# Turning the channels of a scan group by the state's number, in a kernel of two state-space layers

## The chip, the cores and the metric

The kernel runs on one core of a Trainium2 chip. The metric is the device time of one execution in microseconds. A profiled execution gives, beside its time, the span of the work on the core and a trace of every instruction and every DMA packet.

## The reference, cut to what matters

The input `x` is 8 images of 384 channels and 32 x 32 pixels, in float32. Four layers follow one another, each `x = x + layer(group_norm(x))`:

- layer 0: a selective scan over the 1024 pixels (Mamba), 768 inner channels, 16 states each;
- layer 1: a filter in the frequency domain of 8 x 8 blocks, a 3 x 3 convolution by channel and a gate;
- layer 2: a layer norm, the same kind of scan as in layer 0, and an MLP of 384 to 1536 to 384;
- layer 3: a 3 x 3 convolution by channel.

The change lies in the scan of layers 0 and 2. For each inner channel `d` and each state `n`:

```
def step(h, inp):                          # t runs over 1024 pixels
    dt_t, B_t, C_t, u_t = inp
    dA = exp(dt_t[..., None] * A)          # A: [768, 16]
    h = dA * h + (dt_t * u_t)[..., None] * B_t[:, None, :]
    y = einsum('bdn,bn->bd', h, C_t)       # sum over the 16 states
```

So `dt` and `dt * u` are the same for the 16 states of a channel, `B` and `C` are the same for all channels, and `A` differs in both. In which order the channels stand while they are scanned does not matter, so long as `A` and the last sum use the same order.

## The kernel before, in words

**Two phases.** `mamba_phase` runs twice, once for layers 0 and 1, and once for layers 2 and 3. Each goes over 16 chunks: 8 images, each in two halves of `T` = 512 pixels. What a scan needs of the first half it finds in `carry` in the second.

**The scan.** A chunk has 768 channels x 16 states = 12,288 rows of 512 pixels. They are done in 48 steps (`PAIRS`), and a step takes two sets of 128 rows: 8 channels x 16 states on the 128 partitions, the state as the slower index, twice. So `g` and `dA` are tiles of 128 x 2 x 512. A phase has 768 steps, both have 1536.

**The replicas.** A row of `dt` has to stand on 16 partitions, once for each state. `front` therefore computes `dt` (L294) and `du = dt * u` (L297) for 128 channels at a time, and writes each to a tile in DRAM with four DMAs on SP's queue (L302), 32 channels each. The tile is `[2, 32, 2, 512]`: block pair `jp`, channel within a block of 32, block within the pair, pixels. One row of a channel is then 2 x 512 float32, 4 KiB. `begin` (L308) reads back 8 such rows (`E8`), each 16 times, with one DMA of 512 KiB (L313): the source has a first dimension of 16 and step 0. There are two reads in a step, `dtr` from `dtd` and `g` from `dud`, on SP's queue. `dtr` has three buffers and `g` seven. `begin` stands four steps ahead of the scan.

**One step.** In the program's order:

- `begin` issues the two replica reads for step t + 4;
- `times` (L325) multiplies `g` by `B` on POOL for step t + 2;
- `decay` (helper line L96) makes `dA = exp(dtr * A)` on ACT, into PSUM, with two buffers, for step t + 1;
- `scan` (L341) runs two scan instructions on DVE for step t;
- `times` again multiplies by `C`, on DVE for even steps and on POOL for odd ones;
- `gather` (L361) sums over the states on PE: a matmul with the 128 x 32 matrix `sely[:, sub, :]`, which adds the 16 partitions of a channel into the channel's row of `y`.

**What runs between.** Three lanes of other work go on in small pieces between the steps: `front` of the next chunk (in-projection, `dt`, the writes to DRAM), `back` of the current one (gate, L374 to L386), and the end of the chunk before (out-projection L399, then layer 1, or the MLP with weights loaded at L684 and L697, or layer 3). Each engine works through its own instructions in order, and SP's queue issues its DMAs in order. The tile framework sets the final order at build time and puts in the waits; in that order DMAs take eight semaphores in turn, so that a DMA on SP also waits for the one that had its semaphore before.

**Order of channels.** `_constants` builds `sely` with a 1 where partition (n, e) belongs to channel `8 * s + e`, and the host arranges `A_log` to match the partitions.

Of the kernel before, what the change touches and what calls it, by code (L numbers as in the profile page):

```python
# [10 lines left out]
F32 = mybir.dt.float32  # L11
# [5 lines left out]
P = 128  # L17
# [4 lines left out]
ND = DI // P  # L22
NS = 16
# [3 lines left out]
T = 512  # L27
# [8 lines left out]

E8 = 8
NSUB = 4  # L40
PAIRS = [(k, s, jp) for k in range(ND) for s in range(NSUB) for jp in range(2)]
NPAIR = len(PAIRS)
PER_K = NPAIR // ND
# [6 lines left out]
def _flat(ap):  # L50
    return ap.rearrange("p a b -> p (a b)")
# [12 lines left out]
def tile_conv_preact_d4(ctx: ExitStack, tc: tile.TileContext, a: dict, out: bass.AP):  # L64
    nc = tc.nc

    const = ctx.enter_context(tc.tile_pool(name="const", bufs=1))
    dram = ctx.enter_context(tc.tile_pool(name="dram", bufs=1, space=DRAM))
# [33 lines left out]
    sely = const.tile([P, NSUB, 32], F32, name="sely")  # L102
# [82 lines left out]
    def mamba_phase(pre, src, normalise, after_out, tail, load_more, after_chunk=None):  # L185
# [4 lines left out]
        A = w["A"]  # L190
# [16 lines left out]
        def front(s):  # L207

            b, c = s["b"], s["c"]
            if c == 0:  # L210
                s["xn"] = load_half(b, 0)
                stats[b] = yield from group_stats(
                    lambda h, k: s["xn"][:, k, :] if h == 0 else load_block(b, 1, k)
                )
            else:
                s["xn"] = load_half(b, c)
            xn = s["xn"]
            for k in range(KC):
                group_norm(xn[:, k, :], xn[:, k, :], k, stats[b])
            yield  # L220
            if normalise:
                yield from normalise(xn)
            u = s["u"] = wk.tile([P, ND, T], F32, tag="u", name="u", bufs=2)
            xt = xt_of[c] = wk.tile([P, ND, 2], F32, tag="xt", name="xt", bufs=2)
            for d in range(ND):
                ps = yield from ps_tile("ps_in")
                for k in range(KC):
                    nc.tensor.matmul(  # L228
                        ps,
                        w["in"][:, k, d * P : (d + 1) * P],  # L230
                        xn[:, k, :],
                        start=k == 0,
                        stop=k == KC - 1,
                    )
                act(
                    u[:, d, :], ps, AF.Identity, scale=vec[:, d, 2:3], bias=vec[:, d, 3:4]
                )
                if c < NCH - 1:
                    act(xt[:, d, :], ps[:, T - 2 : T], AF.Copy)
                for j in (1, 2):  # L240
                    nc.vector.scalar_tensor_tensor(
                        u[:, d, j:T],
                        ps[:, 0 : T - j],
                        vec[:, d, 2 - j : 3 - j],
                        u[:, d, j:T],
                        ALU.mult,
                        ALU.add,
                    )
                ps_done()
                yield  # L250
            if c > 0:

                prev = xt_of[c - 1]
                hal = wk.tile([P, ND, 3], F32, tag="hal", name="hal")
                nc.gpsimd.tensor_mul(
                    hal[:, :, 0:2], prev, vec[:, :, 0:1].to_broadcast([P, ND, 2])
                )
                nc.gpsimd.tensor_mul(hal[:, :, 2:3], prev[:, :, 1:2], vec[:, :, 1:2])
                nc.gpsimd.tensor_add(hal[:, :, 0:1], hal[:, :, 0:1], hal[:, :, 2:3])
                nc.gpsimd.tensor_add(u[:, :, 0:2], u[:, :, 0:2], hal[:, :, 0:2])  # L260
                yield
            act(_flat(u), _flat(u), AF.Silu)
            yield
            ps = yield from ps_tile("ps_x")
            for d in range(ND):
                nc.tensor.matmul(
                    ps[:RX, :], w["x"][:, d, :], u[:, d, :], start=d == 0, stop=d == ND - 1
                )
            dbc = wk.tile([RX, T], F32, tag="dbc", name="dbc")
            act(dbc, ps[:RX, :], AF.Identity, bias=one_row)  # L270
            ps_done()
            yield
            s["bc"] = wk.tile([P, 2, T], F32, tag="bc", name="bc", bufs=2)
            for j in range(2):
                ps = yield from ps_tile("ps_bc")
                nc.tensor.matmul(ps, selbc[:, j, :], dbc[0:DT0, :], start=True, stop=True)
                act(s["bc"][:, j, :], ps, AF.Copy)
                ps_done()
            yield
            s["dtd"], s["dud"] = [], []  # L280
            for d in range(ND):
                ps = yield from ps_tile("ps_dt")
                nc.tensor.matmul(  # L283
                    ps, w["dt"][DT0:RX, d * P : (d + 1) * P], dbc[DT0:RX, :],
                    start=True, stop=True,
                )

                m = wk.tile([P, T], F32, tag="spm", name="spm", bufs=2)
                act(m, ps, AF.Abs)
                act(m, m, AF.Exp, scale=-1.0)  # L290
                act(m, m, AF.Ln, bias=1.0)
                yield
                dt = wk.tile([P, T], F32, tag="dt", name="dt", bufs=2)
                nc.vector.scalar_tensor_tensor(dt, ps, 0.0, m, ALU.max, ALU.add)  # L294
                ps_done()
                du = wk.tile([P, T], F32, tag="du", name="du", bufs=2)
                nc.gpsimd.tensor_mul(du, dt, u[:, d, :])  # L297
                for name, v in (("dtd", dt), ("dud", du)):
                    to = dram.tile([2, NSUB * E8, 2, T], F32, tag=name, name=name, bufs=2 * ND)
                    s[name].append(to)  # L300
                    for j in range(4):
                        nc.sync.dma_start(  # L302
                            to[j // 2, :, j % 2, :], v[32 * j : 32 * (j + 1), :]
                        )
                yield


        def begin(s, i):  # L308
            k, sub, jp = PAIRS[i]

            def replica(of, tag, bufs):
                t = wk.tile([P, 2, T], F32, tag=tag, name=tag, bufs=bufs)
                nc.sync.dma_start(  # L313
                    _flat(t),
                    of[k][jp, E8 * sub : E8 * (sub + 1)].rearrange("e j t -> e (j t)")
                    .unsqueeze(0).to_broadcast([NS, E8, 2 * T]),
                )
                return t

            s["dtr", i] = replica(s["dtd"], "dtr", 3)  # L320
            s["g", i] = replica(s["dud"], "g", 7)
# [154 lines left out]
        for t in range(total):  # L476
            s, i = steps[t]
# [270 lines left out]
def _constants():  # L748

    ch = np.arange(C) // GS
    group = (ch[:, None] == ch[None, :]) / GS
    y, x = np.meshgrid(np.arange(PS), np.arange(PS), indexing="ij")
    rows, spread = [], []
    for l in range(PS // 2 + 1):
        for k in range(PS):
            phase = 2 * np.pi * (k * y + l * x) / PS
            own = l in (0, PS // 2)  # L760
            if own and k in (0, PS // 2):
                basis = [np.cos(phase) / PS]
            elif own and k > PS // 2:
                continue
            else:
                basis = [np.sqrt(2) * f(phase) / PS for f in (np.cos, np.sin)]
            e = np.zeros((PS, PS // 2 + 1))
            e[k, l] += 0.5 if own else 1.0
            e[-k % PS if own else k, l] += 0.5 if own else 0.0
            for v in basis:  # L770
                rows.append(v)
                spread.append(e.reshape(-1))
    basis = np.stack(rows)
    both = np.zeros((2, PS * PS, PS, 2, PS))
    for i in range(2):
        both[i, :, :, i, :] = basis
    both = both.reshape(P, P)
    spread = np.concatenate([np.stack(spread)] * 2)
    selbc = np.zeros((DT0, 2, NS, E8))
    sely = np.zeros((NS, E8, NSUB, 32))  # L780
    for n in range(NS):
        for j in range(2):
            selbc[j * NS + n, j, n, :] = 1.0
        for e in range(E8):
            for s in range(NSUB):
                sely[n, e, s, E8 * s + e] = 1.0
    one = np.zeros((RX, 1))
    one[DT0] = 1.0
    f = np.float32
    return {  # L790
        "c_group": group.astype(f),
        "c_dft": np.ascontiguousarray(both.T).astype(f),
        "c_idft": both.astype(f),
        "c_spread": np.ascontiguousarray(spread.T).astype(f),
        "c_selbc": selbc.reshape(DT0, 2, P).astype(f),
        "c_sely": sely.reshape(P, NSUB, 32).astype(f),
        "c_one": one.astype(f),
    }
# [68 lines left out]
```

## Time and profile before

| | |
|---|---|
| median of 3 runs | 9624.29 us (9611.26 to 9663.54) |
| profiled execution: time | 9647.44 us |
| profiled execution: span | 9645.6 us |
| granted TensorE clock | 0.757 |
| busy: PE, DVE, ACT, POOL | 65%, 65%, 55%, 59% |
| DMA queue of SP (q1) | 1960.22 MB, 82.4% of 16 engines |
| replica reads (L313) | 2 x 1536 DMAs of 512 KB |
| writes of `dtd` and `dud` (L302) | 2 x 768 DMAs of 64 KB |
| HBM, whole span | 1834.06 MB read, 125.83 MB written |

How to read it: an engine's share is the time in which it executes something, over the span. The DMA share is the time that packets took, summed over the 16 DMA engines, over 16 spans; a packet here is one contiguous piece, 4096 bytes in a replica read, and the small ones are the semaphore updates. A wait is the idle time of an engine before an instruction, under the name of what ended it. "Landing" is the time from the issue of a DMA to its completion.

### The profile page before, as it was taken

How to read it: one execution, taken by the hardware profiler on the slowest of the kernel's cores; microseconds unless marked ns; L12 is line 12 of the kernel's file. 1: busy time of each engine (PE TensorE's matmuls, PEld its weight loads, DVE VectorE, ACT ScalarE, POOL GpSimd, SP SyncE). 2: the span in 40 equal slices, each digit the busy share in tenths (PEclk: the TensorE clock that was granted, in tenths of full speed). 3: DMA queues.
4: the chain of work that ended last, by engine and by line, in shares of the span. 5: the costliest groups of instructions: out<-in, count | busy, mean ns of one | idle time of the engine just before them, and what ended most of it. 6: DMA issues, size and time to landing. Idle time of an engine off the chain costs nothing. (4 is left out here: it accounts for less than half of the span.)

```text
span 9645.6 us, 69137 instructions
## 1 busy us (share of the span) xinstructions
PE 6229.8 (65%) x17410; PEld 2463.2 (26%) x17410; DVE 6273.9 (65%) x6854; ACT 5307.2 (55%) x7051; POOL 5730.9 (59%) x3085
## 2 busy tenths in 40 slices
PE   5566665665556666555557766777666776667765
PEld 1112121211212121111113332333323333233333
DVE  4767676676767667675556576665767656676564
ACT  6776765544546454453446555565555655556552
POOL 3765666666566666665255656556565565665653
PEclk7677676777768677776768877787777887778877
DMA  6988878798887879886478888888888998888885
GB/s 170 228 201 203 213 191 207 187 221 195 200 193 195 206 188 223 195 201 165 117 183 210 221 226 212 210 222 221 223 211 214 221 223 219 210 217 222 223 221 139
DMA packets 631865, 1964.65 MB, mean 204 GB/s; under 512 B 86986, under 2 KB 139130, under 8 KB 631468
## 3 DMA queue, kind: packets, MB, share of 16 engines
q1 hardware_dynamic: 631468, 1960.22, 82.4%
q8 instruction: 143, 2.34, 0.1%
q14 instruction: 254, 2.08, 0.1%
HBM read 1834.06 MB, written 125.83 MB: 203 GB/s over the span
## 5 line engine op out<-in xcount | busy, mean ns | idle before, releaser
L325 POOL TENSOR_TENSOR g<-g,bc 128x1024 f32<-128x1024 f32 x2304 | 5371.0, 2351 | 2279.4 <-DMA g<-dud 1201.9
L361 PE MATMUL y<-g,sely 128*32 128x512 f32 x6144 | 2017.6, 792 | 2262.4 <-POOL g L325 1279.2
L96 ACT ACTIVATE dA<-dtr,w_A 128x512 f32<-128x512 f32 x3072 | 2081.9, 687 | 2324.9 <-DVE g L325 1363.9
L96 ACT ACT_TABLE_LOAD x1201 | 1540.9, 1283 | 164.1 <-DMA dtr<-dtd 52.9
L341 DVE TENSOR_TENSOR_SCAN dA<-dA,carry,g 128x512 f32<-128x512 f32 x768 | 988.0, 1286 | 886.3 <-POOL g L325 499.6
L341 DVE TENSOR_TENSOR_SCAN dA<-dA,g 128x512 f32<-128x512 f32 x768 | 940.8, 1225 | 544.2 <-POOL g L325 322.4
L361 PEld LDWEIGHTS y<-g,sely 128*32 128x32 f32 x6144 | 249.5, 121 | 3647.5 <-POOL g L325 1870.0
L341 DVE TENSOR_TENSOR_SCAN g<-dA,g 128x512 f32<-128x512 f32 x768 | 911.8, 1208 | 260.0 <-POOL g L325 170.8
L341 DVE TENSOR_TENSOR_SCAN g<-dA,carry,g 128x512 f32<-128x512 f32 x768 | 952.2, 1267 | 186.7 <-ACT dA L96 84.6
L325 DVE TENSOR_TENSOR g<-dA,bc 128x1024 f32<-128x1024 f32 x768 | 933.9, 1216 | 8.4
L374 PE MATMUL ps_z<-xf,w_in 128*128 128x512 f32 x1152 | 669.2, 722 | 140.1 <-ACT acc L96 82.6
L686 PE MATMUL ps_up<-t,mw 128*128 128x256 f32 x2304 | 632.5, 427 | 175.3 <-DMA mw<-in_l_mlp_w 91.5
L399 PE MATMUL ps_out<-u,w_out 128*128 128x512 f32 x1152 | 614.5, 691 | 99.2 <-DVE u L386 97.1
L700 PE MATMUL ps_dn<-h,mw 128*128 128x256 f32 x2304 | 560.1, 404 | 131.0 <-DMA mw<-in_l_mlp_w 105.9
L228 PE MATMUL ps_in<-xf,w_in 128*128 128x512 f32 x1152 | 606.3, 671 | 35.2 <-ACT xf L96 16.2
L686 PEld LDWEIGHTS ps_up<-t,mw 128*128 128x128 f32 x2304 | 472.4, 212 | 417.8 <-issue 90.1
L700 PEld LDWEIGHTS ps_dn<-h,mw 128*128 128x128 f32 x2304 | 465.5, 204 | 249.4 <-DVE x L707 72.5
L351 POOL COPY carry<-g 128x2 f32<-128x2 f32 x384 | 72.1, 188 | 729.1 <-DVE g L341 714.2
L283 PE MATMUL ps_dt<-dbc,w_dt 25*128 25x512 f32 x384 | 317.4, 919 | 259.6 <-DVE dt L294 97.9
L297 POOL TENSOR_TENSOR du<-dt,u 128x512 f32<-128x512 f32 x192 | 243.4, 1268 | 361.3 <-DVE dt L294 323.8
L383 DVE SCALAR_TENSOR_TENSOR u<-u,w_vec,y 128x512 f32<-128x512 f32 x192 | 142.4, 742 | 481.5 <-PE y L361 481.4
L374 PEld LDWEIGHTS ps_z<-xf,w_in 128*128 128x128 f32 x1152 | 250.2, 232 | 605.0 <-issue 332.0
(89 smaller groups left out, 5509.1 us busy)
## 6 DMA issues: line engine op xcount, KB each, us to landing
dtr<-dtd SPq DMA_DIRECT2D x1536, 512.0 KB, 7.4
g<-dud SPq DMA_DIRECT2D x1536, 512.0 KB, 8.5
mw<-in_l_mlp_w SPq DMA_DIRECT2D x384, 192.0 KB, 5.4
mw<-in_l_mlp_w SPq DMA_DIRECT2D x96, 768.0 KB, 12.5
dtd<-dt SPq DMA_DIRECT2D x768, 64.0 KB, 3.6
dud<-du SPq DMA_DIRECT2D x768, 64.0 KB, 1.7
xf<-in_x SPq DMA_DIRECT2D x16, 768.0 KB, 7.8
x<-in_x SPq DMA_DIRECT2D x8, 1536.0 KB, 13.2
```

The costliest lines, as they stand in the source:

```text
L96: nc.scalar.activation(out_, in_, func, **kw)
L228: nc.tensor.matmul(ps, w["in"][:, k, d * P : (d + 1) * P], xn[:, k, :], start=k == 0, stop=k == KC - 1,)
L283: nc.tensor.matmul(ps, w["dt"][DT0:RX, d * P : (d + 1) * P], dbc[DT0:RX, :], start=True, stop=True,)
L297: nc.gpsimd.tensor_mul(du, dt, u[:, d, :])
L325: engine.tensor_mul(g, g if in_ is None else in_, s["bc"][:, j, :].unsqueeze(1).to_broadcast([P, 2, T]),)
L341: nc.vector.tensor_tensor_scan(h[:, j, :], dA[:, j, :], g[:, j, :], 0.0 if s["c"] == 0 else carry[:, q : q + 1], ALU.mult, ALU.add,)
L361: nc.tensor.matmul(s["y", k][32 * j : 32 * (j + 1), :], sely[:, sub, :], s["g", i - 1 + j // 2][:, j % 2, :], start=sub == 0, stop=sub == ...
L374: nc.tensor.matmul(ps, w["in"][:, k, DI + d * P : DI + (d + 1) * P], s["xn"][:, k, :], start=k == 0, stop=k == KC - 1,)
L383: nc.vector.scalar_tensor_tensor(u[:, d, :], u[:, d, :], vec[:, d, 4:5], s["y", d], ALU.mult, ALU.add)
L399: nc.tensor.matmul(ps, w["out"][:, d, m * P : (m + 1) * P], s["u"][:, d, :], start=d == 0, stop=d == ND - 1,)
L686: nc.tensor.matmul(ps[:, q, :], wf[:, k, :], s["t"][:, k, cols], start=k == 0, stop=k == KC - 1,)
L700: nc.tensor.matmul(ps[:, :TH], wm[:, f, :], h1[:, f, :], start=f == 0, stop=f == NF - 1,)
```

## The change

Before, the 16 states of a group all read the same 8 channels in the same order. After, state `n` reads the 8 channels that begin `n` places further on, within the block of 32, which is treated as a ring: partition (n, e) of group `sub` holds channel `(8 * sub + n + e) % 32`. Over the four groups every state still meets every channel once.

- `ROT` is the table of those channels. `sely` and the host's arrangement of `A_log` use it. The number and the size of matrices, exponentials, scans and products stay the same.
- The replica read has 4 KiB instead of 0 as the step of its first dimension. It still moves 128 pieces of 4 KiB, from 23 rows where there were 8.
- So that the ring needs no second read at its end, a DRAM tile has 48 rows in place of 32, and the first 16 channels of a block are written a second time behind the 32. That makes eight DMAs for a tile in place of four: 32 channels, then 16, for each of the four blocks.

```diff
+Q = NSUB * E8
+ROT = (8 * np.arange(NSUB)[:, None, None] + np.arange(NS)[:, None] + np.arange(E8)) % Q
...
-                    to = dram.tile([2, NSUB * E8, 2, T], F32, tag=name, name=name, bufs=2 * ND)
+                    to = dram.tile([2, Q + NS, 2, T], F32, tag=name, name=name, bufs=2 * ND)
                     s[name].append(to)
                     for j in range(4):
-                        nc.sync.dma_start(
-                            to[j // 2, :, j % 2, :], v[32 * j : 32 * (j + 1), :]
-                        )
+                        for lo, n in ((0, Q), (Q, NS)):
+                            nc.sync.dma_start(
+                                to[j // 2, lo : lo + n, j % 2, :], v[Q * j : Q * j + n, :]
+                            )
...
                 t = wk.tile([P, 2, T], F32, tag=tag, name=tag, bufs=bufs)
-                nc.sync.dma_start(
-                    _flat(t),
-                    of[k][jp, E8 * sub : E8 * (sub + 1)].rearrange("e j t -> e (j t)")
-                    .unsqueeze(0).to_broadcast([NS, E8, 2 * T]),
-                )
+                rows = of[k][jp, E8 * sub : E8 * (sub + 1)].rearrange("e j t -> e (j t)")
+                turned = bass.AP(
+                    rows.tensor, rows.offset, [[2 * T, NS], [2 * T, E8], [1, 2 * T]]
+                )
+                nc.sync.dma_start(_flat(t), turned)
...
-                sely[n, e, s, E8 * s + e] = 1.0
+                sely[n, e, s, ROT[s, n, e]] = 1.0
...
-        arrays[n + "A"] = np.ascontiguousarray(
-            g[pre + "A_log"].reshape(ND, 4, NSUB, E8, NS).transpose(4, 3, 0, 2, 1)
-        ).reshape(P, 2 * NPAIR)
+        rot = g[pre + "A_log"].reshape(ND, 4, Q, NS)[:, :, ROT, np.arange(NS)[:, None]]
+        arrays[n + "A"] = np.ascontiguousarray(rot.transpose(3, 4, 0, 2, 1)).reshape(
+            P, 2 * NPAIR
+        )
```

## The prediction

> **What bounds the kernel now.** I read the DMA queues first, because the change touches only transfers.
>
> ```profile
> q1 hardware_dynamic: 631468, 1960.22, 82.4%
> ...
> dtr<-dtd SPq DMA_DIRECT2D x1536, 512.0 KB, 7.4
> g<-dud SPq DMA_DIRECT2D x1536, 512.0 KB, 8.5
> ...
> dtd<-dt SPq DMA_DIRECT2D x768, 64.0 KB, 3.6
> dud<-du SPq DMA_DIRECT2D x768, 64.0 KB, 1.7
> ```
>
> The 16 DMA engines are the busiest resource: 82.4%, against 65% for PE and DVE. But 1960.22 MB in 82.4% of 9645.6 us are only 247 GB/s while they work. The replica reads are 3072 x 0.524 = 1611 MB of it. Next, the busy time by stage, one stretch of the start and four of the scans (last three columns: granted clock, DMA share, GB/s).
>
> ```profile
> 26.00:28.00 2.00, 1.73 (x8) 1.73 (x8) 0.35 (x3) 0.00 (x0) 0.00 (x0) 1.00 1.03 416
> 3220.00:3280.00 60.00, 43.16 (x95) 11.91 (x98) 43.38 (x42) 32.52 (x48) 46.88 (x23) 0.79 1.00 225
> 5750.00:5850.00 100.00, 81.21 (x260) 38.63 (x258) 76.10 (x76) 62.01 (x87) 68.66 (x33) 0.90 1.00 254
> 7440.00:7500.00 60.00, 40.18 (x114) 15.07 (x114) 39.24 (x36) 25.54 (x36) 41.08 (x20) 0.72 1.01 248
> 9380.00:9460.00 80.00, 52.80 (x166) 22.39 (x164) 56.57 (x53) 38.42 (x49) 56.91 (x25) 0.77 1.01 242
> ```
>
> At 26 us the queue holds a plain load of `x`, whose 384 rows of 4 KiB are read once each: 416 GB/s at a full queue. In the scans the queue is as full and moves 225 to 254 GB/s. The packet records agree: a 4096-byte packet of that load takes 159 ns (median), a packet of the scans 278 ns (mean 271). Same size, same kind of target; what differs is that each row is asked for by 16 partitions at once, and that the core is loaded. In the four scan stretches (300 us) DVE is busy 72% and POOL 71%, so the queue, not an engine, sets the pace there. Counted over the trace, the DMA share is at least 0.96 in 3600 us (windows of 20 us) to 4550 us (windows of 10 us): I take 4000 us. Third, the waits.
>
> ```profile
> POOL g L325 <- DMA g<-dud: 1201.9, 430, 11.5
> ...
> ACT dA L96 <- DMA dtr<-dtd: 451.1, 154, 8.1
> ```
> ```profile
> SPq L313 <- ACT dA L96: 3001.5, 868, 14.6
> SPq L313 <- PE y L361: 823.2, 268, 12.1
> ...
> SPq L302 <- DVE dt L294: 589.5, 110, 57.0
> ```
>
> POOL and ACT stand idle 1653 us, in 584 waits, for a replica to land. SP is mostly early: it waits 3001.5 us for ACT to free a buffer of `dtr`. Where it stops for `dt` (110 times), it is late for what stands behind.
>
> [...]
>
> **The change part by part.**
>
> *Replica packets.* 3072 x 128 = 393,216 packets on 16 engines: at 271 ns, 6660 us of queue. Lower bound 159 ns, as at the start. Upper bound 271 ns, no gain; more would need 23 rows to be worse than 8, which I exclude nearly, since the plain load reads 384 rows at full rate. Between: the 6144-byte packets of weights take 234 ns at the start and 260 (median) to 312 (mean) over the whole trace, so load costs 1.11 to 1.33 times. 159 x 1.11 to 1.33 is 177 to 212 ns; I take 190. Queue time falls by 393,216 x 81 / 16 = 1990 us, to about 4670.
>
> *Added writes.* 1536 more DMAs, 24,576 packets of 2048 bytes at 109 ns (mean of that size): 167 us of queue, and 16 semaphore packets each at 14 ns: 21 us. The queue then holds 7948 - 1990 + 188 = 6146 us of packets, 64% of the old span. It is no longer the tightest resource.
>
> *Saturated stretches.* There the same work would need 0.70 of the queue's time (190 / 271). The engines come next: from 0.72 busy they cannot go to 1, because DVE, ACT, POOL and PE pass each step on in order (DVE frees the PSUM buffer that ACT waits for, 1363.9 us in all). I take 0.82: 4000 x (1 - 0.72 / 0.82) = 490 us saved. Bounds: 0.76 gives 210, 0.88 gives 730.
>
> *The other 5650 us.* A replica lands in 4.2 us at the least; its own 8 packets per engine are 8 x 0.271 = 2.2 us, so 2.0 us are fixed. Of the median 7.4 and 8.5, some 5.4 to 6.5 scale with packets; at 0.70 that is 1.6 to 2.0 us earlier. Applied to the 584 waits it is up to 1050 us of engine idle, part of it in the stretches counted already, and much of it beside other idle time. I take 150 us here, bounds 0 and 400.
>
> *SP's queue.* The trace has a block with `dt` late:
>
> ```profile
> 3027.26 1.71 SPq L302 DMA_DIRECT2D dtd<-dt  x4
> 3029.07 1.77 SPq L302 DMA_DIRECT2D dud<-du  x4
> 3030.94 0.52 SPq L313 DMA_DIRECT2D g<-dud  x1
> ```
> ```profile
> 3035.71 2.35 POOL L325 TENSOR_TENSOR g<-g,bc 128x1024 f32<-128x1024 f32 x1 [7.14 <-DMA g<-dud]
> ```
>
> Four writes take 1.71 us to issue, so a block's eight more take 3.45 us, and the replica behind them, for which POOL idled 7.14 us here, starts that much later. Over 192 blocks it is 662 us of SP. Where SP is early this hides behind the 3001.5 us; if that cover goes, all 662 show. On the path I count the 110 blocks in which SP had waited for `dt`: 110 x 3.45 = 380 us, less the earlier landing, 110 x 1.8 = 200: 180 us lost. Each write also waits for the eighth DMA before it. The ninth write comes 8 x 0.43 = 3.45 us after the first, which lands after 3.6 (`dtd`) or 1.7: no stall by the medians; behind a full queue up to a replica's 8.5 - 3.45 = 5 us. Bounds 0 and 660 us.
>
> *At no cost.* `ROT`, `sely` and `A` change values only: instruction counts and shapes are the same. The compiled order of PE, ACT and POOL shifts by a few matmuls, except in the first chunk (up to some 20); I count 0, bounds -50 and +50 (half a per cent, as it hits one chunk of 32 hardest).
>
> Sum: -490 - 150 + 180 = -460 us on the profiled 9647 us, which stands 23 us above the median of the runs. So 9187 by the profile, 9164 against the median; I round to 9160.
>
> **Rivals.**
>
> 1. *The engines take over earlier or later* (faster, other size). With both savings at their lower bounds and 180 lost, -30 to -100: about 9550. With the upper bounds, -730 - 400 + 180: about 8680. For the first speaks that stretches with a DMA share near 0.8 show DVE no busier (0.6) than the full ones; for the second, 3001.5 us in which SP waits to be let go.
> 2. *SP's write bursts become the wait* (slower). Sixteen writes in a row hold the two replicas behind them, `dtr` for ACT and `g` for POOL, in all 192 blocks. Against savings of 640 us it decides when a block loses over 640 / 192 = 3.3 us after its earlier landing, that is, when both the 3.45 us of issue and an eight-DMA stall of over 1.7 us show everywhere. With the full 5 us of stall: 192 x (3.45 + 5.0 - 1.8) = 1280, and 9624 + 640 = 10,260; with half the stall, 192 x 4.15 = 800: 9780, which I take. Against it: SP is mostly early.
> 3. *The rows are not what slows the packets* (slower; the change doesn't do what it says). They stay near 271 ns because of load on HBM and SBUF. Then the 188 us of queue and 180 to 380 us of SP are pure cost: about 9850. Against it: weight packets under the same load lose only 11 to 33%, replicas 70%.
>
> **How the numbers follow.** A measurement of this kernel can tell about 0.5% (48 us) from no change. Chances: forecast, 8850 to 9400: 0.60; larger gain, below 8850: 0.12; smaller gain, 9400 to 9576: 0.11; within 0.5%: 0.05; rival 2: 0.05; rival 3: 0.07. Faster 0.83, same 0.05, slower 0.12. The range 8720 to 9600 leaves out about 0.06 below and 0.14 above.
>
> **What would show it.** Right: scan packets near 190 ns, full stretches above 320 GB/s, q1's share between 60 and 72% of a shorter span, landings of `dtr` and `g` near 5.5 to 6.5 us, POOL's wait for `g` well below 1201.9 us, DVE's and POOL's shares up to 68% and 62%. SP's waits at L302 on DMAs should grow little. Wrong: packets still at 270 ns (rival 3); packets faster but POOL waiting more for `g` behind L302 (rival 2); or both waits down and PE's or DVE's waits for one another up by as much (rival 1's small gain).

## The result, and the profile after

The changed kernel takes **10,534.94 us** (median of 4 runs, 10,518.49 to 10,541.98) against 9617.78 us of the kernel before on the same chip: a ratio of 1.0942, with a 95% interval of 1.0903 to 1.0981. It is 917 us slower. The forecast was 9160 us, with a range up to 9600.

The profiled execution has a span of 10,536.4 us. First the DMA queues and landings on the page of the changed kernel:

```profile
q1 hardware_dynamic: 680620, 2010.65, 76.7%
...
dtr<-dtd SPq DMA_DIRECT2D x1536, 512.0 KB, 6.9
g<-dud SPq DMA_DIRECT2D x1536, 512.0 KB, 8.2
...
dtd<-dt SPq DMA_DIRECT2D x768, 64.0 KB, 2.8
dud<-du SPq DMA_DIRECT2D x768, 64.0 KB, 1.7
dtd<-dt SPq DMA_DIRECT2D x768, 32.0 KB, 1.7
dud<-du SPq DMA_DIRECT2D x768, 32.0 KB, 1.7
```

2010.65 MB in 76.7% of the span are 249 GB/s, where there were 247. A 4096-byte packet takes 275 ns (median; mean 267) where it took 278 (mean 271). So the turned read is as slow as the old one, and the share is lower only because the span is longer. The waits of ACT, POOL and DVE in the changed kernel, longest first:

```profile
ACT dA L99 <- DVE g L329: 1911.2, 385, 8.6
...
POOL carry L355 <- DVE g L345: 1366.8, 298, 16.3
DVE dA L345 <- POOL g L329: 1326.6, 296, 9.0
...
POOL g L329 <- DMA g<-dud: 934.2, 346, 18.8
...
ACT dA L99 <- DMA dtr<-dtd: 512.4, 142, 10.3
```

POOL's wait for `g` to land fell from 1201.9 us to 934.2 and ACT's for `dtr` rose from 451.1 to 512.4. What grew is the wait of one engine for another: `dA` on ACT for DVE by 547 us, the carry on POOL for DVE by 653, the scan on DVE for POOL by 505. In the kernel before these three were:

```profile
ACT dA L96 <- DVE g L325: 1363.9, 351, 11.3
...
DVE dA L341 <- POOL g L325: 822.0, 204, 6.5
POOL carry L351 <- DVE g L341: 714.2, 219, 11.7
```

And the waits on SP's queue in the changed kernel:

```profile
SPq L321 <- ACT dA L99: 3671.9, 898, 23.4
...
SPq L306 <- DVE dt L297: 303.0, 66, 56.2
...
SPq L306 <- DMA g<-dud: 198.1, 121, 2.5
SPq L306 <- DMA dtr<-dtd: 136.1, 114, 2.9
```

At L306 SP waits 334 us for replicas to land, because a write has to wait for the DMA that had its semaphore before (in the trace each of SP's DMAs has the semaphore of the eighth before it). In the kernel before it was 221 us:

```profile
SPq L302 <- DMA g<-dud: 139.8, 89, 2.2
...
SPq L302 <- DMA dtr<-dtd: 80.8, 72, 2.7
```

SP waits for `dt` 303.0 us, less than the 589.5 before, which fits a queue that is itself later.

Two stretches show what happened. Here is SP's queue in the changed kernel, start and length in us:

```profile
2692.77 5.20 SPq L306 DMA_DIRECT2D dtd<-dt  x8
2698.36 3.55 SPq L306 DMA_DIRECT2D dud<-du  x8
2705.48 3.56 SPq L306 DMA_DIRECT2D dtd<-dt  x8
2709.14 3.62 SPq L306 DMA_DIRECT2D dud<-du  x8
2719.30 3.55 SPq L306 DMA_DIRECT2D dtd<-dt  x8
2722.94 4.96 SPq L306 DMA_DIRECT2D dud<-du  x8
2730.66 3.55 SPq L306 DMA_DIRECT2D dtd<-dt  x8
2734.30 3.62 SPq L306 DMA_DIRECT2D dud<-du  x8
2738.02 0.52 SPq L321 DMA_DIRECT2D g<-dud  x1
```

64 writes stand in a row. Each block's writes take over 7 us, and SP waits in between for the next block's `dt`; the replica at 2738 us waits behind all four. The scans stand still for it: in most even chunks of layer 0 their steps 24 and 25 take some 41 us longer than before, in those of layer 2 steps 34 and 35 some 33 us. A part of that is made up in the steps that follow. In the compiled order such runs of 64 occur 13 times, and each kernel has two places with all six blocks in a row; apart from these the kernel before has at most 24 writes in a row (three blocks).

The second stretch is POOL's, near the end of a chunk of the changed kernel:

```profile
2866.09 0.18 POOL L355 COPY carry<-g 128x2 f32<-128x2 f32 x1 [4.07 <-DVE g L345]
2866.35 6.95 POOL L329 TENSOR_TENSOR g<-g,bc 128x1024 f32<-128x1024 f32 x3
2877.23 0.18 POOL L355 COPY carry<-g 128x2 f32<-128x2 f32 x1 [3.93 <-DVE g L345]
2877.50 6.94 POOL L329 TENSOR_TENSOR g<-g,bc 128x1024 f32<-128x1024 f32 x3
```

Three products, then a wait for DVE's scan of the odd step, then three products again: 11.1 us for two steps, with POOL and DVE taking turns. No DMA ends a wait here. The reason is the order of POOL's queue: the C product of an odd step (which needs that step's scan) stands ahead of the next B product (which DVE's next scan needs). I call that a **turn-taking place**. Counted in the compiled order, the changed kernel has 371 of them among 768, the kernel before 250. In the same part of the chunk before, two steps took 6 to 9.6 us.

### The profile page after: what moved, and what is told of

It reads as the page before. It is cut to its first block, busy times and chain, and to the rows that moved or that the text cites. A ratio compares the mean times of both kernels' runs of the same rounds, so it can differ in the third digit from the quotient of the medians.

```text
span 10536.4 us, 71155 instructions
## 1 busy us (share of the span) xinstructions
PE 6390.8 (61%) x17410; PEld 2481.5 (24%) x17410; DVE 6319.1 (60%) x6854; ACT 5201.4 (49%) x6957; POOL 5725.3 (54%) x3085
## 3 DMA queue, kind: packets, MB, share of 16 engines
q1 hardware_dynamic: 680620, 2010.65, 76.7%
## 5 line engine op out<-in xcount | busy, mean ns | idle before, releaser
L365 PE MATMUL y<-g,sely 128*32 128x512 f32 x6144 | 2125.9, 829 | 2829.2 <-POOL g L329 1427.4
L403 PE MATMUL ps_out<-u,w_out 128*128 128x512 f32 x1152 | 643.2, 718 | 121.3 <-DVE u L390 121.3
```

The lines of the kernel that those rows point to most:

```text
L365: nc.tensor.matmul(s["y", k][32 * j : 32 * (j + 1), :], sely[:, sub, :], s["g", i - 1 + j // 2][:, j % 2, :], start=sub == 0, stop=sub == ...
L403: nc.tensor.matmul(ps, w["out"][:, d, m * P : (m + 1) * P], s["u"][:, d, :], start=d == 0, stop=d == ND - 1,)
```

## Experiments

Theory A: the turn does nothing for the packets, and the added writes on SP cost the time. Theory B: the rows matter, one way or the other. Each experiment is measured against the kernel before on its own chip, at 9622 to 9636 us.

**1. Loads alone.** What sets a packet's time?

```diff
+PATTERNS = [
+    ("same", [[0, 16], [L, 8], [1, L]]),
+    ("turned", [[L, 16], [L, 8], [1, L]]),
+    ("apart", [[9 * L, 16], [L, 8], [1, L]]),
+    ("plain", [[L, P], [1, L]]),
+    ("onerow", [[0, P], [1, L]]),
+    ("four", [[0, 32], [L, 4], [1, L]]),
...
```

> Nothing but loads: eight stages of eight DMAs of 512 KiB each from x in HBM to 128 partitions, in 4 KiB pieces, one stage after the other; the layers are left out and the output is zeros. The stages differ in the source alone: 'same' (16 times 8 rows, first dimension 16 with step 0), 'turned' (step one row), 'apart' (step nine rows, 128 different rows), 'plain' (128 rows, first dimension 128), 'onerow' (one row for all partitions, first dimension 128), 'four' and 'fourturned' (first dimension 32), 'two' (first dimension 64). Theory A, what sets a packet's time is [...], and that follows from the first dimension: same, turned and apart all near 275 ns and 240 GB/s though they read 8, 23 and 128 rows; plain and onerow near 160 ns and 400 GB/s. Theory B, rows shared by engines are slow: same and onerow slow, apart and plain fast, turned between. Theory C, an idle chip reads everything fast and it is the load of the scans that slows packets: all near 160 ns.

The middle of each stage, in the order of the list, with DMA share and GB/s as the last two columns; engines and clock stand before them:

```profile
4.00:20.00 16.00, 0.00 (x0) 0.00 (x0) 1.00 1.03 232
25.00:40.00 15.00, 0.00 (x0) 0.00 (x0) 1.00 1.03 238
45.00:60.00 15.00, 0.00 (x0) 0.00 (x0) 1.00 1.03 241
66.00:74.00 8.00, 0.00 (x0) 0.00 (x0) 1.00 1.01 387
80.00:90.00 10.00, 0.00 (x0) 0.00 (x0) 1.00 1.02 296
96.00:104.00 8.00, 0.00 (x0) 0.00 (x0) 1.00 1.02 370
110.00:119.00 9.00, 0.00 (x0) 0.00 (x0) 1.00 1.02 374
125.00:133.00 8.00, 0.00 (x0) 0.00 (x0) 1.00 1.02 369
```

8, 23 or 128 rows with a first dimension of 16: 232, 238 and 241 GB/s, median packets of 299, 296 and 292 ns. A first dimension of 32, 64 or 128: 369 to 387 GB/s and 159 ns. So with nothing else running, the form of the read decides and the sharing of rows hardly does. Only 'onerow', one row for all 128 partitions, pays for sharing: 296 GB/s, 185 ns; there theory A missed. Theory C is out: the old form is slow without any load of the scans.

Why the first dimension decides is not shown: the trace gives a packet's queue, size and times and no more. That it decides is shown, by 232 to 241 GB/s with 16 against 369 to 374 with 32 and 64, where both groups hold reads that repeat rows.

**2. The turned read alone**, in the kernel before.

```diff
-                    .unsqueeze(0).to_broadcast([NS, E8, 2 * T]),
+                turned = bass.AP(
+                    rows.tensor, rows.offset - back, [[2 * T, NS], [2 * T, E8], [1, 2 * T]]
+                )
```

> The kernel before with the turned read alone: step 4 KiB instead of 0 in the source of the replica, writes as before (32 rows, four DMAs a tile). The rows read are not those that A and the sums stand for, so the scan runs on other channels; the work is the same. SP's order is that of the kernel before. Theory A (the turn does nothing for the packets, the writes cost the time): packets stay at 270 to 280 ns and the time within 0.5% of before, 9620. Theory B (the turn itself harms or helps the reads): the packets move by over 10 ns and the time with them; if the turn made the loss, 10,500.

9610.22 us, ratio 0.9987 (0.9978 to 0.9997); packets 275 ns, mean 268. The turn brings 0.1%. In the traces every engine and SP's queue go through their instructions in the same order as in the kernel before.

**3. The second writes alone**, in the kernel before.

```diff
-                        nc.sync.dma_start(
-                            to[j // 2, :, j % 2, :], v[32 * j : 32 * (j + 1), :]
-                        )
+                        for lo, n in ((0, 32), (32, NS)):
+                            nc.sync.dma_start(
+                                to[j // 2, lo : lo + n, j % 2, :], v[32 * j : 32 * j + n, :]
+                            )
```

> The kernel before with the second writes alone: DRAM tiles of 48 rows, eight write DMAs a tile; the replica reads stay as before with step 0 and never touch the 16 added rows. The computation is whole. SP's order is that of the changed kernel. Theory A (the added writes on SP's queue cost the time): 10,450 to 10,600, as the changed kernel. Theory B (the turned read costs it): about 9620 to 9800.

10,535.99 us, ratio 1.0965 (1.0947 to 1.0984). This is the whole loss, without the turn. Here the traces have the same order as the changed kernel's on every engine and on SP, so the two differ in the turn alone: 10,534.94 and 10,535.99 us.

**4. The second writes on POOL's queue**, in the changed kernel.

```diff
-                            nc.sync.dma_start(
+                            (nc.sync if lo == 0 else nc.gpsimd).dma_start(
```

> The changed kernel with the second writes (16 rows, 1536 DMAs) on POOL's queue; the first writes and the reads stay on SP's. SP's order is then that of the kernel before, with runs of 8 writes instead of 16 to 96 between replicas, while the same bytes and DMAs go through the 16 engines. Theory A1 (the place and order on SP's queue cost the time): most of the 917 us comes back, 9650 to 9950, the rest being POOL's time to issue. Theory A2 (the load of 1536 more DMAs on the 16 engines costs it, wherever they are issued): 10,300 or more.

9538.13 us, ratio 0.9923 (0.9908 to 0.9938): slightly faster than before, and below the range of theory A1. The same bytes and the same number of DMAs go through the 16 engines, so their load is not the cost. Off SP's queue the writes cost nothing. But two things went with them: the issue time on SP, and the order that the framework makes, which is here that of before on SP and has 232 turn-taking places on POOL.

**5. and 6. SP in the program's order**, in the changed kernel, and in a kernel with two writes a block (below).

```diff
+    def pinned(dst, src):
+        tc.keep_in_program_order(nc.sync.dma_start(dst, src))
```

> The changed kernel with one thing more: each write of dtd and dud and each replica read keeps the program's place in the SP queue, so that the queue alternates 16 writes with replica pairs in 180 of 182 places and never holds 64 writes in a row. Number, bytes and issue time of the DMAs are those of the changed kernel. Theory A1 (the loss is the order: replicas placed behind the writes of up to four blocks, whose dt comes late): the stall of 33 to 42 us in every second chunk goes, 9600 to 9900. Theory A2 (the loss is 1536 more issues of 0.43 us on SP, in any order): 10,300 to 10,550.

10,966.97 us, ratio 1.1396 (1.1369 to 1.1423). A miss for both theories. The program's order is not the old order: the runs of 64 are gone, but SP now waits 676.7 us for `dt` with replicas behind, where the changed kernel waits 303.0, and turn-taking places rise to 469. With two writes a block and the same kind of order it is 10,030.30 us.

> The one-write kernel with writes and replica reads kept in the program's place on SP's queue (two writes, then replicas, in 180 of 182 places). If the framework's own order costs time before the change too: 30 to 250 us below the one-write kernel. If not: the same time within 0.5%, or slower where SP now waits for dt with a replica ready behind it.

Ratio 1.0421 (1.0394 to 1.0449), slower than its own kernel by 453 us: not the hoped-for gain but the second case of the expectation, with SP waiting 960.2 us for `dt` against 589.5 in that kernel. The difference of the two, 937 us for 2688 writes, is 0.35 us for a write, where the trace has 0.42 us for its issue (median). That is a hint that issue time counts and no more, because the two also differ in POOL's order and in the sums (see 8).

**7. Faster packets alone**, in the kernel before: would the forecast have held if the packets had done their part?

```diff
-                    .unsqueeze(0).to_broadcast([NS, E8, 2 * T]),
+                four = bass.AP(rows.tensor, rows.offset, [[0, 32], [2 * T, 4], [1, 2 * T]])
```

> The kernel before with another source of the replica read alone: 4 rows, 32 times (first dimension 32), instead of 8 rows 16 times. Bytes, number and size of the packets, DMAs, buffers and SP's order are those of the kernel before; half of the channels are left out of the scan and the others done twice. The load stages gave 159 ns for this form and 299 for the old one. Theory A (the DMA queue sets the pace where its share is 1.0, as the prediction reckoned): packets 160 to 200 ns, queue share near 60%, and the time falls by 400 to 700 us, to 8900 to 9200. Theory D (the engines hold one another in order, the full queue is only what they leave waiting): packets as fast, the time falls by less than 150 us, 9480 to 9620.

9306.77 us, ratio 0.9671 (0.9645 to 0.9697): 330 us, short of theory A and beyond theory D. The page of this kernel:

```profile
q1 hardware_dynamic: 631468, 1960.22, 60.9%
...
dtr<-dtd SPq DMA_DIRECT2D x1536, 512.0 KB, 4.6
g<-dud SPq DMA_DIRECT2D x1536, 512.0 KB, 5.3
```

Packets take 159 ns (median; mean 186), and a replica lands 3 us earlier. The kernel reads 4 rows where there were 8, and by the load stages the number of rows makes little difference (232 GB/s for 8 rows and 241 for 128 with a first dimension of 16; 370 for 4 and 374 for 35 with 32). The longest waits of ACT and POOL are then those for DVE:

```profile
ACT dA L96 <- DVE g L323: 1504.0, 404, 8.8
...
POOL g L323 <- DVE g L339: 949.5, 272, 11.9
...
POOL g L323 <- DMA g<-dud: 667.3, 247, 10.4
```

**8. One write a tile.** The DRAM tile is `[128, 512]` in the channels' own order.

```diff
-                    to = dram.tile([2, NSUB * E8, 2, T], F32, tag=name, name=name, bufs=2 * ND)
+                    to = dram.tile([P, T], F32, tag=name, name=name, bufs=2 * ND)
...
+                    nc.sync.dma_start(to, v)
...
-                    of[k][jp, E8 * sub : E8 * (sub + 1)].rearrange("e j t -> e (j t)")
+                    of[k][32 * sub + 16 * jp : 32 * sub + 16 * (jp + 1)]
+                    .rearrange("(e j) t -> e (j t)", j=2)
```

> The kernel before with fewer writes: the DRAM tile is [128, 512] in the channels' own order and is written with one DMA of 128 partitions instead of four of 32; a replica reads 8 pairs of neighbouring channels, 16 times, step 0; A and the matrix of the sums are arranged to match. The computation is whole. 384 writes instead of 1536. If SP's issue time or its order bounds the kernel before too: 9300 to 9550. If SP is early everywhere that matters: within 0.5% of 9620.

9577.46 us, ratio 0.9946 (0.993 to 0.9963): 59 us, close to the second case. Fewer writes bring little under the framework's own order. The 59 us are not theirs alone: in this layout the four sums of a pair of steps go to the same 32 rows of PSUM instead of four different ones, PE is busy 7056.0 us instead of 6229.8, and the granted clock is 0.849 instead of 0.757.

**9. and 10. POOL's order, exchanged.** The sequence of POOL's 2304 products is read from the compiled order of one kernel and kept in the other by edges without waits, that is, orders for the framework that add no semaphore.

```diff
+    for which in f"{int(POOL_ORDER, 16):02304b}":
+        ins = products[int(which)].popleft()
+        if before is not None:
+            tc.add_manual_dep(ins, before.name, ...)
+        before = ins
```

> The kernel before, with POOL's 2304 products of g kept in the order that they have in the compiled changed kernel (328 of the 2304 places differ); writes and reads are those of before, SP still has 8 writes between replicas in 123 of 150 places. In the changed kernel's order 371 of the 768 C products of odd states stand ahead of the next B product, against 250 before, so that POOL and DVE take turns (11.1 us for two steps where other stretches take 6 to 8). Theory P (POOL's order is a large part of the loss): 121 more such places at some 3.5 us are 420 us, 9950 to 10,150; if it were the whole loss, 10,500. Theory S (only SP's runs of 64 writes cost the time): within 0.7% of 9620.

9959.66 us, ratio 1.035 (1.0334 to 1.0366): 332 us from POOL's order with not one DMA added. The wait that belongs to it, in this kernel, was 822.0 us before:

```profile
DVE dA L353 <- POOL g L335: 1250.0, 322, 8.5
```

> The changed kernel, with POOL's products of g kept in the order of the compiled kernel before; SP's queue still holds 64 writes in a row in 13 places. Theory P, part of the loss: 10,000 to 10,200, with the single stall of 33 to 42 us in every second chunk still there (14 x 38 = 530 us). Theory P, whole loss: 9620 to 9700. Theory S: 10,450 to 10,600, as the changed kernel.

10,344.58 us, ratio 1.0744 (1.0726 to 1.0762): less came back (190 us) than was expected. The order is a part of the loss, and here the smaller one. The result lies in no range that was set: above theory P's, below theory S's.

**11. and 12. Both orders, exchanged**, to tell the order on SP from the time of issue: writes and reads on SP kept in the other kernel's sequence in the same way, together with POOL's.

```diff
+    chain(zlib.decompress(base64.b64decode(SP_ORDER)).decode(), moves)
+    chain(f"{int(POOL_ORDER, 16):02304b}", {"0": products[0], "1": products[1]})
```

> The changed kernel, all 3072 writes on SP, with the order of POOL's products and the order of writes and replica reads on SP's queue both kept as in the compiled kernel before (each write there is two writes here: at most 48 in a row before the first scan and in the middle, mostly 16). Theory O (the two orders are the loss, the issue of 1536 more DMAs hides behind SP's waits): within 1.5% of the kernel before, 9600 to 9760. Theory I (SP's issue time is the larger part of what POOL's order leaves unexplained, 580 to 730 us): 10,150 to 10,350.

10,396.87 us, ratio 1.0791 (1.0763 to 1.0818). With both orders of before, the 1536 added writes cost 761 us, 0.50 us each. Three waits of this kernel (L139 and L101 are its helper lines of `act` and of the moves on SP) show where:

```profile
ACT dA L139 <- DMA dtr<-dtd: 993.4, 273, 9.7
```
```profile
SPq L101 <- DMA dtr<-dtd: 519.9, 360, 6.2
...
SPq L101 <- DMA g<-dud: 278.1, 178, 2.6
```

ACT waits 993.4 us for `dtr`, where it was 451.1 before. SP itself waits 798 us for earlier replicas to land, against 561 (311.4 + 29.1 at L313, 139.8 + 80.8 at L302): 237 us on top of 1536 x 0.42 = 645 us of issue.

> The kernel before, 1536 writes, with both orders kept as in the compiled changed kernel (runs of 32 writes in 13 places, which there are 64). Theory O: 10,350 to 10,550, nearly the changed kernel's 10,535. Theory I: 9950 to 10,050, as with POOL's order alone (9960).

10,077.32 us, ratio 1.0456 (1.0435 to 1.0477): both orders of the changed kernel, without its writes, cost 442 us. Theory I is near on both, 47 us and 27 us above its ranges, theory O far off on both. The six kernels together, as differences to the kernel before on the same chip:

| writes on SP | POOL's order | SP's order | us |
|---|---|---|---|
| 1536 | before | before | 0 |
| 1536 | after | near that of before | +332 |
| 1536 | after | after | +442 |
| 3072 | before | before | +761 |
| 3072 | before | near that of after | +717 |
| 3072 | after | after | +917 |

Down one path the loss is 332 for POOL's order, 110 for SP's order and 475 for the writes; down another it is 761 for the writes and 156 for the orders. The parts overlap, and their sizes depend on what is already there. Down both paths the writes on SP are the larger part.

One rival is left. The two sequences that were kept are POOL's products and SP's writes and replica reads; the framework still ordered DVE, ACT and PE by itself. In the trace of the kernel with both orders of before, 2533 of DVE's 6854 instructions stand at another place than in the kernel before (1390 of 5546 on ACT, table loads left out), about as many as in the changed kernel (2590 and 1376). How much of the 761 us is their order, and how much SP's issue time and waits, was not tried.

**13. and 14. POOL's products in the program's order**, C always behind the B products of three more steps (764 of 768 places), in the kernel before and in the one-write kernel.

```diff
+            if engine is nc.gpsimd:
+                in_turn_of(ins)      # an edge without a wait to the product before it
```

> The kernel before, with POOL's products of g kept in the program's order: the C product of an odd state always stands behind the B products of the next three steps (764 of 768 places). If the taking of turns between POOL and DVE costs the kernel before as well (250 places at some 3.5 us are 870 us): 8800 to 9300. If a product held for a replica that is late costs as much: 9500 to 9900.

9307.31 us, ratio 0.9668 (0.9647 to 0.9688): between the two cases, 320 us gained. POOL's wait for DVE's scan, 893.6 us in the kernel before, is nearly gone:

```profile
POOL g L337 <- DVE g L355: 98.9, 35, 6.6
```

Late replicas take part of the gain back, as POOL's wait for `g` shows: 1464.8 us against 1201.9.

> The one-write kernel (9577) with POOL's products kept in the program's order. Fewer places to gain (186 instead of 250) but replicas that are less held up by writes on SP: 8750 to 9250 if the turns are what costs; 9450 to 9800 if late replicas take their place.

**8956.99 us**, ratio 0.93 (0.9273 to 0.9326): faster than both kernels, with the whole computation. Here the layout with 1152 fewer writes is worth 350 us against the kernel above (0.30 us a write, if it were the writes alone), where under the framework's order it was worth 59; the other sums of 8 and the higher clock (0.840 against 0.759 here, 0.849 against 0.757 in 8) are in both figures. Its DMA queue is fuller than that of any other kernel here that has the layers:

```profile
q1 hardware_dynamic: 613036, 1960.15, 86.8%
```

## Why the prediction was wrong, step by step

- *Replica packets, 190 ns taken, 159 to 271 as bounds.* **This step failed.** They stayed at 267 (mean), nearly the upper bound. The comparison with the load of `x` was sound, but I put the difference down to shared rows, when the two reads also differ in the first dimension of the source. The load stages separate them: 'apart' shares no row and is as slow as 'same'. That states 4 KiB apart would be read faster I assumed; no trace had shown it, and the step alone left the packets where they were (a mean of 268 ns against 271, experiment 2).
- *SP's queue, 180 us taken, 0 to 660 as bounds.* **This step failed by its size.** The mechanism was named: eight more issues a block and the semaphore of the eighth DMA before. Measured, it is 475 to 761 us, with the order of DVE, ACT and PE not held. The mistake was to count only the 110 blocks in which SP had waited for `dt`, and to credit an earlier landing that didn't come. The 3001.5 us that SP waits for a buffer were taken as cover, but they were not used up: they rose to 3671.9 us, while the writes stood in runs of 64. SP is early between the blocks and late in them. The forecast had pictured 16 writes in a row.
- *Order of the compiled queues, 0 taken, 50 us either way as bounds.* **This step failed.** Two orders that differ in 328 of POOL's 2304 product places are 332 us apart. I looked at how far instructions had moved, not at what stood ahead of what, and left DVE out, where 2590 of 6854 instructions moved.
- *Saturated stretches and the rest, 490 + 150 us.* Not tested by the change itself, since the packets didn't get faster. With packets at 186 ns in the same order (experiment 7) it is 330 us: about half. The two traces can be compared scan step by scan step. The steps that lay where the queue was full (3554 us, by windows of 20 us) take 209 us less, just the lower bound of the 490, and DVE's busy share in them rises from 0.71 to 0.75 and not to 0.82; all other steps take 140 us less, near the 150. So a full queue does set the pace, but the engines take over sooner than I took.
- *Added writes on the DMA engines, 188 us of queue.* Right in size (76.7% of 10,536.4 us is 8081 us of packets, 133 more than before, with each replica packet 4 ns shorter), and right that they don't count: with the second writes on POOL's queue the kernel is no slower than before (ratio 0.9923).
- *The rivals.* Rival 3's outcome came true (packets stay), but not its reason: with nothing else running the same packets take 292 to 299 ns, so it is not the load of the scans. Rival 2 (SP's bursts hold the replicas) came true in the 64 writes and in SP's waits for DMAs at the writes, 334 us against 221, but not by its sign: POOL waits less for `g`, and the engines more for one another. I priced each as if the other did not come. Rival 3 took only 180 to 380 us for SP; rival 2 set its price against savings of 640 us and took off an earlier landing. Without both, its sum is 9624 + 192 x 3.45 = 10,286 for issue alone and 9624 + 192 x (3.45 + 2.5) = 10,766 with half the stall; the measured 10,535 lies between. Rival 1's lower case is -30 us by its own terms; nothing in them gives the -100.

## What to carry to other kernels

Before a slow transfer is put down to where its rows lie, compare it with a fast one of the same size in everything that differs, the first dimension of the access pattern above all (here 232 to 241 GB/s with 16, 369 to 374 with 32 and 64): a small kernel of loads settles it in one run. Count what a change adds to an in-order DMA queue in issues as well as in bytes (here 0.42 us an issue), and price it in the stretch where the queue is late; waits of the same queue elsewhere were no cover here (3001.5 us before, 3671.9 in the kernel that was 917 us slower). Where a framework sets the order, one more DMA can change what stands ahead of what on an engine that it doesn't touch (here 371 turn-taking places on POOL for 250), so look for pairs in which a result that is needed late was put ahead of one that is needed now.

## What the runs showed of the hardware that was not expected

- A read of 128 pieces of 4 KiB whose source has 16 as its first dimension moves 232 to 241 GB/s; with 32, 64 or 128 it moves 369 to 387 GB/s. With the same first dimension, how many different rows it reads makes less than 10 GB/s of difference, except for one row read by all partitions (296 against 387 GB/s).
- The granted TensorE clock was 0.849 in the one-write kernel against 0.757 before, with more busy time on PE (7056.0 us against 6229.8). Its sums write other PSUM rows; whether that is the reason was not tried.
- Left open: why the added writes cost 0.50 us each with the old orders and 0.31 with the new ones, and whether a layout with 32 as its first dimension can hold the whole computation. The six kernels show only that the parts overlap, and the order of DVE, ACT and PE was not held in them.
